# Attention and involution in one kernel: closing steps that wait for operand and bank, and a last chunk whose tap weights TensorE makes

## The chip, the cores and the metric

The kernel runs on one core of one Trainium2 chip. The core has TensorE (PE, matrix products into PSUM), VectorE (DVE), ScalarE (ACT), GpSimd (POOL) and SyncE (SP, which here only issues DMAs), each with its own instruction stream in a fixed order, and 16 DMA engines. An instruction that waits holds up all that stand behind it on its engine. The metric is the device time of one execution in microseconds.

## The reference

The input x is (4, 512, 64, 64) in float32. Two layers follow each other, each with its input added to its output.

```python
# layer 0: self-attention over the 4096 positions, 128 inner channels
q, k, v = wq x + bq, wk x + bk, wv x + bv
attn = softmax(q^T k)
x = wo (v attn^T) + bo + x
# layer 1: involution, 7 x 7 taps, groups of 16 channels
o1 = relu(s1 * (W1 x) + b1)                 # 512 -> 128 channels
w  = Ws relu(sr * (Wr o1) + br) + bs        # 128 -> 32 -> 8 groups x 49 taps
acc[c] = sum over taps of w[c // 16, tap] * o1[c] shifted by the tap
x = s3 * (W3 acc) + b3 + x                  # 128 -> 512 channels
```

## The kernel before

A batch (there are four) is worked in three kinds of stages. `keys_values` makes the keys and the transposed values of all 4096 positions. `attention` then takes 8 chunks of 512 queries; for each it runs through 32 tiles of 128 keys. In one such iteration PE makes a score tile `pss` for two iterations ahead, ACT takes its exponential into `pt`, PE adds `v` times `pt` to `po`, and DVE adds `pt` to `pacc` for the softmax sums. [...]

All else that a chunk needs is done by generators that the attention of the next chunks steps once an iteration, through `chores()`:

- `finish_chunk`: ACT copies `po` to `on`; PE spreads the sums over all partitions (`pl`); DVE takes four reciprocals `rl` (L327) and multiplies `on` by `rl` (L330); four matmuls `pwo` give the output projection, which DVE adds to the x chunk `xb` (L337); four matmuls into `p1` and ACT (L353) give `o1`; ACT adds b3 to `xb` (L365); `pr` and ACT (L371) give `red`, the 32 reduced channels repeated in four row groups; four matmuls `pc` of 32 rows each and ACT (L386) give `wc`, the 392 weights of the taps of every position. SP writes `wc` to a scratch in DRAM (`wsp`, L393). From there seven broadcast loads `wb` of 1792 KB (seven taps each; `pump`, L171) bring every group's weights to its 16 channels. The pool `wb` has three buffers, and at most two pieces are issued ahead.
- `involution`: for each of the 49 taps DVE multiplies the shifted `o1` (kept in PSUM as `po1`) by its weights (L215), and POOL adds the product to `acc` (L229). Products go to a pool of seven buffers. Taps from 28 on need rows of the next chunk's `o1` and wait until that is noted in `ready`.
- `close_chunk`: four matmuls `py` with W3, which DVE adds to `xb` (L246), and the store of the chunk (L252).

PSUM gives two banks to the tag `mm`, which `pl`, `pwo`, `p1`, `pr`, `pc`, `py` and `pq` share in turn; two to `pss` and `pk`; and one each to `po`, `pacc` and `po1`.

The order of the instructions is laid down when the kernel is built. A planner keeps a clock `pe` of the matmuls issued so far, and in `free` the time to which each other engine is booked. A generator that yields comes again in the next iteration, and the yields in `finish_chunk` and `close_chunk` are fixed in number. `pace()` meters the taps (0.70 a microsecond of `pe`), and a tap is held back while its piece, by the planner's figures (`PIECE_US` 7.4 a piece), has not landed, or while DVE or POOL is booked too far ahead. The framework's scheduler may then still move instructions on an engine.

After the last batch's attention comes the tail, where nothing is left to lay beside the steps: finishing, closing and taps are stepped three, three and two at a time. There PE takes a part of the additions: of the odd taps up to 45 it adds the product to `accp` by a matmul with the identity, and DVE adds `accp` to `acc` at the end (L232). A last check of the sums decides whether a general path, which doesn't run with these inputs, must compute everything again.

Of the kernel before, what the change touches and what calls it, by code (L numbers as in the profile page):

```python
# [8 lines left out]
F32 = mybir.dt.float32  # L9
# [40 lines left out]


PE_COLUMN = 0.43 / 256
DVE_OP, POOL_OP = 0.7, 1.28
PIECE_US, X_US, WC_US, LAND_US = 7.4, 3.8, 3.6, 3.5

SAFE = (1e-30, 1e20)

# [2 lines left out]
def fast_path(  # L60
# [46 lines left out]

    finishing, closing, taps = [], [], []  # L110
    pe = 0.0
    due, seen = 0.0, 0.0
    free = {"dve": 0.0, "pool": 0.0, "dma": 0.0}
    ready = set()
    pending, loaded = [], []

# [4 lines left out]
    def takes(engine, us):  # L121
        free[engine] = max(free[engine], pe) + us
        return free[engine]

    def load_x(kind, b, c):
        xt = xpool.tile([P, CT, CH], F32, tag="x", name=f"{kind}_{b}_{c}")
# [58 lines left out]
    def involution(b, c, o1):  # L185
        top = RW + PAD

        po1 = ps1.tile([P, RW + 2 * PAD, W + 2 * PAD], F32, tag="o1", name=f"po1_{b}_{c}")
        for _ in range(2):
            yield "wait"  # L190
        nc.scalar.copy(po1[:, :top], o1[:, :top])
        yield "wait"
        acc = work2.tile([P, RW, W], F32, tag="acc", name=f"acc_{b}_{c}")
        accp = None
        for tap in range(NTAP):
            dy, dx = divmod(tap, K)
            if dx == 0:
                if dy == PAD + 1:
                    while (b, c) not in ready:
                        yield "wait"  # L200
                    yield "wait"
                    nc.scalar.copy(po1[:, top:], o1[:, top:])
                    yield "wait"
                wb, landed = loaded.pop(0)
                pump()
            while "tail" not in ready and (
                pe < landed or free["dve"] > pe + 3.0 or free["pool"] > pe + 6.0
            ):
                yield "wait"
            free["pool"] = max(free["pool"], takes("dve", DVE_OP))  # L210
            takes("pool", POOL_OP)
            prod = acc
            if tap:
                prod = prods.tile([P, RW, W], F32, tag="prod", name=f"prod_{b}_{c}_{tap}")
            nc.vector.tensor_tensor(  # L215
                prod, po1[:, dy : dy + RW, dx : dx + W],
                wb[:, dx, :].rearrange("p (r w) -> p r w", r=RW), ALU.mult,
            )
            if tap and "tail" in ready and tap % 2 and tap < NTAP - 2:

                first = accp is None
                if first:
                    accp = ps1.tile([P, CH], F32, tag="po", name=f"accp_{b}_{c}")
                mm(
                    accp, ident, prod.rearrange("p r w -> p (r w)"),
                    start=first, stop=tap == NTAP - 4,
                )
            elif tap:
                nc.gpsimd.tensor_tensor(acc, acc, prod, ALU.add)  # L229
            yield  # L230
        if accp is not None:
            nc.vector.tensor_tensor(  # L232
                acc, accp.rearrange("p (r w) -> p r w", r=RW), acc, ALU.add
            )
        closing.append(close_chunk(b, c, acc))


    def close_chunk(b, c, acc):
        xt = xb[b, c]
        for _ in range(5):  # L240
            yield
        for t in range(CT):
            py = ps.tile([P, CH], F32, tag="mm", name=f"py_{b}_{c}_{t}")
            mm(py, w_slice(O_W3, t), acc.rearrange("p r w -> p (r w)"))
            takes("dve", DVE_OP)
            nc.vector.scalar_tensor_tensor(  # L246
                xt[:, t, :], py, v1(V_S3 + t), xt[:, t, :], ALU.mult, ALU.add
            )
            for _ in range(2):
                yield  # L250
        takes("dma", X_US)
        nc.sync.dma_start(out_r[b, :, :, c * CH : (c + 1) * CH], xt)  # L252
        del xb[b, c]
# [40 lines left out]
    def queries(b, c):  # L294
        xt = xb[b, c]
        pq = ps.tile([P, CH], F32, tag="mm", name=f"pq_{b}_{c}")
        for t in range(CT):
            mm(pq, w_slice(O_WQ, t), xt[:, t, :], t == 0, t == CT - 1)
        q = work2.tile([P, CH], F32, tag="q", name=f"q_{b}_{c}")
        nc.scalar.activation(q, pq, AF.Identity, bias=v1(V_BQ))  # L300
        return q

# [11 lines left out]
    def finish_chunk(b, c, o1s, po, sums):  # L314
        xt = xb[b, c]
        on = work2.tile([P, CH], F32, tag="on", name=f"on_{b}_{c}")
        nc.scalar.copy(on, po)
        for _ in range(3):
            yield
        pl = ps.tile([P, CH], F32, tag="mm", name=f"pl_{b}_{c}")  # L320
        mm(pl, ones, sums)
        rl = work1.tile([P, CH], F32, tag="rl", name=f"rl_{b}_{c}")
        for i in range(4):
            yield
            cols = slice(i * P, (i + 1) * P)
            takes("dve", 0.9)
            nc.vector.reciprocal(rl[:, cols], pl[:, cols])  # L327
        nc.sync.dma_start(rls[b * NCH + c : b * NCH + c + 1, :], rl[:1, :])
        takes("dve", DVE_OP)
        nc.vector.tensor_tensor(on, on, rl, ALU.mult)  # L330
        for _ in range(2):
            yield
        for t in range(CT):
            pw = ps.tile([P, CH], F32, tag="mm", name=f"pwo_{b}_{c}_{t}")
            mm(pw, w_slice(O_WO, t), on)
            takes("dve", DVE_OP)
            nc.vector.scalar_tensor_tensor(  # L337
                xt[:, t, :], pw, bo[:, t : t + 1], xt[:, t, :], ALU.add, ALU.add
            )
            yield  # L340
            if t % 2:
                yield
        p1 = ps.tile([P, RW, W], F32, tag="mm", name=f"p1_{b}_{c}")
        for t in range(CT):
            mm(
                p1.rearrange("p r w -> p (r w)"), w_slice(O_W1, t), xt[:, t, :],
                t == 0, t == CT - 1,
            )
            if t == 1:
                yield  # L350
        o1 = o1s[c]
        inner = o1[:, PAD : PAD + RW, PAD : PAD + W]
        nc.scalar.activation(inner, p1, AF.Relu, bias=v1(V_B1), scale=v1(V_S1))  # L353
        if c + 1 < NCH:
            o1s[c + 1] = new_o1(b, c + 1)
            nc.gpsimd.tensor_copy(  # L356
                o1s[c + 1][:, :PAD, PAD : PAD + W], o1[:, RW : RW + PAD, PAD : PAD + W]
            )
        if c > 0:
            nc.gpsimd.tensor_copy(  # L360
                o1s.pop(c - 1)[:, PAD + RW :, PAD : PAD + W], o1[:, PAD : 2 * PAD, PAD : PAD + W]
            )
        for t in range(CT):

            nc.scalar.activation(xt[:, t, :], xt[:, t, :], AF.Identity, bias=v1(V_B3 + t))  # L365
            if t % 2:
                yield
        pr = ps.tile([P, CH], F32, tag="mm", name=f"pr_{b}_{c}")
        mm(pr, wt[:, O_WR : O_WR + P], inner)
        red = work1.tile([P, CH], F32, tag="red", name=f"red_{b}_{c}")  # L370
        nc.scalar.activation(red, pr, AF.Relu, bias=v1(V_BR), scale=v1(V_SR))  # L371
        for _ in range(2):
            yield
        wc = work1.tile([P, 4, CH], F32, tag="wc", name=f"wc_{b}_{c}")
        for m0 in range(0, 4, 2):
            pcs = []
            for m in range(m0, m0 + 2):

                pc = ps.tile([P, CH], F32, tag="mm", name=f"pc_{b}_{c}_{m}")
                mm(  # L380
                    pc[:NWC, :], wt[CR * m : CR * (m + 1), O_WC : O_WC + NWC],
                    red[CR * m : CR * (m + 1), :], shared=2,
                )
                pcs.append(pc)
            for m, pc in zip(range(m0, m0 + 2), pcs):
                nc.scalar.activation(  # L386
                    wc[:NWC, m, :], pc[:NWC, :], AF.Identity,
                    bias=vec[:NWC, V_BC + m : V_BC + m + 1],
                )
            yield  # L390
        wsp = scratch.tile([4 * NWC, CH], F32, tag="wsp", name=f"wsp_{b}_{c}")
        written = takes("dma", WC_US) + LAND_US
        nc.sync.dma_start(wsp.rearrange("(m r) n -> r m n", m=4), wc[:NWC])  # L393
        pending.extend((wsp, written, i, f"wb_{b}_{c}_{i}") for i in range(NTAP // PIECE))
        pump()
        if c > 0:
            ready.add((b, c - 1))
        if c == NCH - 1:
            ready.add((b, c))
        taps.append(involution(b, c, o1))  # L400


    def attention(b, kt, vT):
# [5 lines left out]
        def score(n):  # L409
            c, j = divmod(n, nj)  # L410
            pss = ps.tile([P, CH], F32, tag="s", name=f"pss_{b}_{c}_{j}")
            mm(pss, kt[:, j * P : (j + 1) * P], qs[c])
            pt = ptpool.tile([P, CH], F32, tag="pt", name=f"pt_{b}_{c}_{j}")
            nc.scalar.activation(pt, pss, AF.Exp)  # L414
            pts[n] = pt

# [2 lines left out]
        for n in range(NCH * nj):  # L419
# [3 lines left out]
                paccs[c] = ps1.tile([P, CH], F32, tag="acc", name=f"pacc_{b}_{c}")  # L423
            if j == 14 and c + 1 < NCH:
                xb[b, c + 1] = load_x("xb", b, c + 1)
            if j == 8 and c == NCH - 1 and b + 1 < B:
                for i in range(2):
                    xa[b + 1, i] = load_x("xa", b + 1, i)
# [19 lines left out]
    for b in range(B):  # L448
        kv = keys_values(b)
        if b == 0:  # L450
# [3 lines left out]
                mm(pb[:, t : t + 1], w_slice(O_WO, t), v1(V_BVC))  # L454
            bo = const.tile([P, CT], F32, name="bo")
            nc.vector.tensor_tensor(bo, pb, vec[:, V_BO : V_BO + CT], ALU.add)
        attention(b, *kv)
    ready.add("tail")
    while finishing or closing or taps:
        step(finishing, 3)  # L460
        step(closing, 3)
        step(taps, 2)


    ok = const.tile([B * NCH, CH], F32, name="ok")
# [395 lines left out]
```

## Time and profile before

| what | us |
| --- | --- |
| median of three runs | 2900.23 |
| lowest and highest run | 2894.04, 2903.88 |
| the profiled execution's own time | 2898.7 |
| its span, first to last instruction | 2896.9 |
| PE busy | 2702.9 |
| DVE busy | 1919.7 |
| POOL busy | 1916.3 |
| ACT busy | 954.5 |
| last `po` matmul ends | 2760.5 |

The mean granted TensorE clock over the span was 0.972. The DMA engines moved 540.84 MB, of which the 224 pieces of `wb` are the most. In the lists below, a line of groups gives code line, engine, operation, destination and sources, shapes, count, then busy time and the mean ns of one, and the idle time before the group with what ended it. A line of a timeline gives start and duration in microseconds, and in brackets how long the engine had been idle and what released it.

### The profile page before, as it was taken

What the parts mean: (1) busy time and instruction counts of PE and PEld (TensorE: products, weight loads), DVE (VectorE), ACT (ScalarE), POOL (GpSimd) and SP (SyncE); (2) the same over time, 40 slices, a digit from 0 to 9 for tenths busy, and PEclk for the clock granted to TensorE, in tenths of its full rate; (3) what the DMA queues carried; (4) which work ended last, traced back from release to release, by engine and by line L of the source; (5) the groups of instructions that cost most, each with busy time, mean ns of one, the idle gap of its engine ahead of it and who ended that gap; (6) DMA issues with size and microseconds to landing.
All of it is one profiled execution on the core that took longest, in us unless ns stands there. A gap on an engine that the chain in (4) does not pass through costs nothing.

```text
span 2896.9 us, 23193 instructions
## 1 busy us (share of the span) xinstructions
PE 2702.9 (93%) x6250; PEld 1150.1 (40%) x6250; DVE 1919.7 (66%) x3016; ACT 954.5 (33%) x1569; POOL 1916.3 (66%) x1623
## 2 busy tenths in 40 slices
PE   8999999999899999999989999999989999999975
PEld 4444443343344444443434444443334444444421
DVE  0447777876456777777464777777636577777864
ACT  2333333332233333333223333333233333333310
POOL 0028877777734877887780777778865288777744
PEclk9999999999999999999999999999999999999987
DMA  6048888889937988888991989998895588888896
GB/s 213 15 100 180 205 202 194 202 200 226 237 84 183 198 199 202 199 202 203 253 215 41 213 199 207 204 202 206 213 242 139 123 201 201 201 189 189 188 229 167
DMA packets 97532, 540.84 MB, mean 187 GB/s; under 512 B 6640, under 2 KB 6768, under 8 KB 68592
## 3 DMA queue, kind: packets, MB, share of 16 engines
q1 hardware_dynamic: 97104, 538.01, 79.5%
q8 instruction: 51, 0.84, 0.1%
q10 hardware_dynamic: 288, 1.27, 0.1%
q14 instruction: 89, 0.73, 0.1%
HBM read 479.94 MB, written 59.24 MB: 186 GB/s over the span
## 4 chain that ended last, share of the span: by engine, by line
PE 37%; DMA 33%; POOL 14%; DVE 10%; issue 5%; ACT 1%; SPq 0%; POOLq 0%; DVEq 0%; ACTq 0%
DMA wb<-wsp 31%; POOL acc L229 13%; PE pss L147 11%; PE po L147 11%; PE py L147 4%; DVE pacc L439 4%; PE p L147 4%; DVE prod L215 3%; PE pwo L147 3%; DVE rl L327 2%; DMA wsp<-wc 2%; PE pv L147 1%; PE pk L147 1%; PE pq L147 1%; DMA out_dram<-xb 0%
## 5 line engine op out<-in xcount | busy, mean ns | idle before, releaser
L229 POOL TENSOR_TENSOR acc<-acc,prod 128x512 f32<-128x512 f32 x1488 | 1889.9, 1270 | 462.5 <-DVE prod L215 317.7
L215 DVE TENSOR_TENSOR prod<-po,wb 128x512 f32<-128x512 f32 x1536 | 1001.0, 681 | 281.5 <-DMA wb<-wsp 200.9
L147 PE MATMUL pss<-q,k 128*128 128x512 f32 x2048 | 1070.5, 605 | 34.5 <-ACT pt L414 34.5
L147 PE MATMUL po<-pt,v 128*128 128x512 f32 x2048 | 1063.0, 602 | 0.0
L414 ACT ACTIVATE pt<-pss 128x512 f32<-128x512 f32 x1024 | 610.5, 597 | 1255.1 <-PE pss L147 1128.4
L439 DVE TENSOR_TENSOR pacc<-pacc,pt 128x512 f32<-128x512 f32 x960 | 662.1, 690 | 289.9 <-ACT pt L414 287.1
L147 PEld LDWEIGHTS pss<-q,k 128*128 128x128 f32 x2048 | 387.2, 192 | 555.2 <-issue 485.0
L147 PEld LDWEIGHTS po<-pt,v 128*128 128x128 f32 x2048 | 393.0, 193 | 506.0 <-issue 487.9
L356 POOL COPY o<-o 128x192 f32<-128x192 f32 x28 | 9.7, 348 | 463.2 <-ACT o L353 317.4
L147 PE MATMUL pwo<-on,wt 128*128 128x512 f32 x256 | 143.1, 643 | 80.6 <-DVE on L330 78.3
L246 DVE SCALAR_TENSOR_TENSOR xb<-py,vec,xb 128x512 f32<-128x512 f32 x128 | 95.4, 745 | 100.5 <-PE py L147 99.7
L147 PE MATMUL py<-acc,wt 128*128 128x512 f32 x256 | 136.5, 620 | 22.1 <-DVE xb L337 12.1
L215 DVE TENSOR_TENSOR acc<-po,wb 128x512 f32<-128x512 f32 x32 | 22.1, 692 | 187.9 <-DMA wb<-wsp 187.8
L147 PE MATMUL pk<-xa,wt 128*128 128x512 f32 x256 | 122.7, 618 | 3.5 <-DMA xa<-x_dram 3.5
L365 ACT ACTIVATE xb<-xb,vec 128x512 f32<-128x512 f32 x128 | 91.9, 718 | 91.9 <-PE p L147 87.4
L147 PE MATMUL p<-xb,wt 128*128 128x512 f32 x256 | 120.1, 592 | 0.0
L147 PE MATMUL pv<-xa,wt 128*128 128x512 f32 x256 | 118.3, 600 | 0.0
L327 DVE RECIPROCAL rl<-pl 128x128 f32<-128x128 f32 x128 | 115.6, 929 | 1.6 <-PE pl L147 1.6
L147 PE MATMUL pq<-xb,wt 128*128 128x512 f32 x256 | 115.7, 592 | 0.0
L147 PEld LDWEIGHTS pwo<-on,wt 128*128 128x128 f32 x256 | 50.5, 207 | 160.2 <-DVE on L330 101.2
L386 ACT ACTIVATE wc<-pc,vec 98x512 f32<-98x512 f32 x128 | 81.2, 684 | 80.1 <-PE pc L147 80.1
L337 DVE SCALAR_TENSOR_TENSOR xb<-pwo,bo,xb 128x512 f32<-128x512 f32 x128 | 94.5, 740 | 14.8 <-PE pwo L147 14.5
(50 smaller groups left out, 822.2 us busy)
## 6 DMA issues: line engine op xcount, KB each, us to landing
wb<-wsp SPq DMA_DIRECT2D x224, 1792.0 KB
xa<-x_dram SPq DMA_DIRECT2D x32, 1024.0 KB
xb<-x_dram SPq DMA_DIRECT2D x32, 1024.0 KB
out_dram<-xb SPq DMA_DIRECT2D x32, 1024.0 KB
wsp<-wc SPq DMA_DIRECT2D x32, 784.0 KB
wt<-wts_dram ACTq DMA_DIRECT2D x1, 1137.0 KB
wt<-wts_dram SPq DMA_DIRECT2D x1, 512.0 KB
rls<-rl SPq DMA_DIRECT2D x32, 2.0 KB
```

The source lines that it names most:

```text
L147: nc.tensor.matmul(o, lhsT=lhsT, rhs=rhs, start=start, stop=stop)
L215: nc.vector.tensor_tensor(prod, po1[:, dy : dy + RW, dx : dx + W], wb[:, dx, :].rearrange("p (r w) -> p r w", r=RW), ALU.mult,)
L229: nc.gpsimd.tensor_tensor(acc, acc, prod, ALU.add)
L246: nc.vector.scalar_tensor_tensor(xt[:, t, :], py, v1(V_S3 + t), xt[:, t, :], ALU.mult, ALU.add)
L327: nc.vector.reciprocal(rl[:, cols], pl[:, cols])
L337: nc.vector.scalar_tensor_tensor(xt[:, t, :], pw, bo[:, t : t + 1], xt[:, t, :], ALU.add, ALU.add)
L356: nc.gpsimd.tensor_copy(o1s[c + 1][:, :PAD, PAD : PAD + W], o1[:, RW : RW + PAD, PAD : PAD + W])
L365: nc.scalar.activation(xt[:, t, :], xt[:, t, :], AF.Identity, bias=v1(V_B3 + t))
L386: nc.scalar.activation(wc[:NWC, m, :], pc[:NWC, :], AF.Identity, bias=vec[:NWC, V_BC + m : V_BC + m + 1],)
L414: nc.scalar.activation(pt, pss, AF.Exp)
L439: nc.vector.tensor_tensor(paccs[c], paccs[c], pt, ALU.add)
```

## The change

The planner's fixed yields in `finish_chunk`, `close_chunk` and `involution` give way to two conditions. `until(time)` yields until the planner's clock has reached a time, by which it reckons the operand to be ready. `bank()` does the same for the next bank of the tag `mm`: a list `banks` holds the times at which the two banks are reckoned to come free. ACT has an account of its own, and 0.3 us are reckoned for a hop between engines. In `finish_chunk` the b3 copies now stand behind `red`, the note in `ready` comes before the weights are made, and the four `pc` are laid down in two adjacent pairs.

The last chunk of the last batch has a way of its own, `involution_last`. It makes no `wc`, no scratch and no pieces. For each tap PE makes the weights of all 128 channels at once from 32 rows of `red` and a table `ws` into the two banks of `pss`; DVE adds the bias and multiplies by the shifted `o1` in one instruction; 33 of the products are added by PE through the identity into `accp`, and 15 by POOL. The table is loaded in batch 3 into one of the six buffers of the pool `x` and keeps it to the end. The tail runs the finishing to its end first, and then steps two taps of the last chunk for one of the chunk before it, all of whose additions are now POOL's.

```diff
-    free = {"dve": 0.0, "pool": 0.0, "dma": 0.0}
+    free = {"dve": 0.0, "pool": 0.0, "act": 0.0, "dma": 0.0}
+    banks = [0.0, 0.0]
...
+    def until(us, sign=None):
+        while pe < us and "tail" not in ready:
+            yield sign
+
+    def bank():
+        yield from until(banks[0])
+        banks.pop(0)
...
-            if tap and "tail" in ready and tap % 2 and tap < NTAP - 2:
...
-            elif tap:
+            if tap:
                 nc.gpsimd.tensor_tensor(acc, acc, prod, ALU.add)
...
+    def involution_last(b, c, o1, red):
+        acc = work2.tile([P, RW, W], F32, tag="acc", name="acc_last")
+        accp = ps1.tile([P, RW, W], F32, tag="po", name="accp")
+        by_pe = [tap for tap in range(1, NTAP - 4) if tap % 4]
+        late = []
+
+        def add(tap, prod):
+            if tap in by_pe:
+                mm(
+                    accp.rearrange("p r w -> p (r w)"), ident, prod.rearrange("p r w -> p (r w)"),
+                    tap == by_pe[0], tap == by_pe[-1],
+                )
+            else:
+                nc.gpsimd.tensor_tensor(acc, acc, prod, ALU.add)
+
+        for tap in range(NTAP):
+            r0 = CR * (tap % 4)
+            dy, dx = divmod(tap, K)
+            pw = ps.tile([P, RW, W], F32, tag="s", name=f"pw_{tap}")
+            mm(
+                pw.rearrange("p r w -> p (r w)"),
+                ws[r0 : r0 + CR, tap // 4 * P : (tap // 4 + 1) * P], red[r0 : r0 + CR, :],
+            )
...
+            nc.vector.scalar_tensor_tensor(
+                prod, pw, v1(V_BS + tap), o1[:, dy : dy + RW, dx : dx + W], ALU.add, ALU.mult
+            )
+            if tap:
+                late.append((tap, prod))
+            if len(late) > 2:
+                add(*late.pop(0))
+            yield
+        for tap, prod in late:
+            add(tap, prod)
+        nc.vector.tensor_tensor(acc, accp, acc, ALU.add)
+        closing.append(close_chunk(b, c, acc))
...
     def close_chunk(b, c, acc):
         xt = xb[b, c]
-        for _ in range(5):
-            yield
+        yield from until(free["pool"] + HOP_US)
         for t in range(CT):
+            yield from bank()
             py = ps.tile([P, CH], F32, tag="mm", name=f"py_{b}_{c}_{t}")
             mm(py, w_slice(O_W3, t), acc.rearrange("p r w -> p (r w)"))
-            takes("dve", DVE_OP)
+            banks.append(takes("dve", DVE_OP) + HOP_US)
...
     def finish_chunk(b, c, o1s, po, sums):
...
+        takes("act", ACT_OP)
         nc.scalar.copy(on, po)
-        for _ in range(3):
-            yield
+        yield from until(free["dve"] + HOP_US)
+        yield from bank()
         pl = ps.tile([P, CH], F32, tag="mm", name=f"pl_{b}_{c}")
...
+        banks.append(free["dve"] + HOP_US)
         nc.sync.dma_start(rls[b * NCH + c : b * NCH + c + 1, :], rl[:1, :])
-        takes("dve", DVE_OP)
         nc.vector.tensor_tensor(on, on, rl, ALU.mult)
-        for _ in range(2):
-            yield
+        yield from until(takes("dve", DVE_OP) + HOP_US)
         for t in range(CT):
+            yield from bank()
             pw = ps.tile([P, CH], F32, tag="mm", name=f"pwo_{b}_{c}_{t}")
             mm(pw, w_slice(O_WO, t), on)
-            takes("dve", DVE_OP)
+            banks.append(takes("dve", DVE_OP) + HOP_US)
...
+        if (b, c) == (B - 1, NCH - 1):
+            taps_last.append(involution_last(b, c, o1, red))
+            return
+        yield from until(made)
         wc = work1.tile([P, 4, CH], F32, tag="wc", name=f"wc_{b}_{c}")
...
+            if (b, c, j) == (B - 1, 5, 0):
+                nc.sync.dma_start(ws, wts[:, O_WS:])
...
+        if b == B - 1:
+            ws = xpool.tile([P, CT * CH], F32, tag="x", name="ws")[:, : NWT - O_WS]
         attention(b, *kv)
     ready.add("tail")
-    while finishing or closing or taps:
-        step(finishing, 3)
-        step(closing, 3)
-        step(taps, 2)
+    while finishing:
+        step(finishing, 1)
+        step(closing, 1)
+        step(taps, 1)
+    while closing or taps or taps_last:
+        step(taps_last, 2)
+        step(taps, 1)
+        step(closing, 1)
```

## The prediction

> **What bounds the kernel now.** I read the page's first part and its chain first, then the waits, then the timelines of one chunk in the steady part, and last the tail.
>
> Page, parts 1, 4 and 5 (busy us, share of the span, count; the chain's shares; a group's busy and mean ns, then the idle time before it):
> ```profile
> PE 2702.9 (93%) x6250; PEld 1150.1 (40%) x6250; DVE 1919.7 (66%) x3016; ACT 954.5 (33%) x1569; POOL 1916.3 (66%) x1623
> ...
> PE 37%; DMA 33%; POOL 14%; DVE 10%; issue 5%; ACT 1%; SPq 0%; POOLq 0%; DVEq 0%; ACTq 0%
> ...
> L229 POOL TENSOR_TENSOR acc<-acc,prod 128x512 f32<-128x512 f32 x1488 | 1889.9, 1270 | 462.5 <-DVE prod L215 317.7
> L215 DVE TENSOR_TENSOR prod<-po,wb 128x512 f32<-128x512 f32 x1536 | 1001.0, 681 | 281.5 <-DMA wb<-wsp 200.9
> ```
> PE is nearly full, yet DMA holds a third of the chain: it is a loop through several engines that sets the period. The waits (total, times, longest):
> ```profile
> DVE prod L215 <- DMA wb<-wsp: 200.9, 82, 7.4
> DVE acc L215 <- DMA wb<-wsp: 187.8, 31, 22.9
> ...
> PE pwo L147 <- DVE on L330: 78.3, 27, 3.6
> ```
> Timeline of DVE in one chunk (start, us, instruction, idle before it):
> ```profile
> 1982.32 0.69 DVE L215 TENSOR_TENSOR acc<-po,wb 128x512 f32<-128x512 f32 x1 [4.23 <-DMA wb<-wsp]
> ...
> 1990.91 0.69 DVE L215 TENSOR_TENSOR prod<-po,wb 128x512 f32<-128x512 f32 x1 [1.92 <-DMA wb<-wsp]
> ...
> 1999.46 0.69 DVE L215 TENSOR_TENSOR prod<-po,wb 128x512 f32<-128x512 f32 x1 [1.89 <-DMA wb<-wsp]
> ...
> 2001.27 1.76 DVE L327 RECIPROCAL rl<-pl 128x128 f32<-128x128 f32 x2
> ...
> 2006.41 0.68 DVE L330 TENSOR_TENSOR on<-on,rl 128x512 f32<-128x512 f32 x1
> ```
> and of PE:
> ```profile
> 2007.14 1.13 PE L147 MATMUL pwo<-on,wt 128*128 128x512 f32 x2 [2.87 <-DVE on L330]
> ...
> 2012.08 1.10 PE L147 MATMUL py<-acc,wt 128*128 128x512 f32 x2 [1.24 <-DVE xb L337]
> ```
> DVE works in the order that was laid down, so it sits at the first product of the third wb piece until that lands (1999.46); the reciprocals stand behind that product, `on` behind them, and PE at pwo behind `on`. The pieces land 8.6 us apart; 224 pieces took 1914 us of DMA time, 8.55 each. The loop closes: pwo to the issue of wsp 37.1 us (a PE stretch), to wb_0's issue 4.4, to the third landing 28.3, to pwo 7.7: 77.5 us, which is the period (77.3 to 79.4 in most chunks) against 72.2 us of PE work (84 matmuls by 0.86). The excess of chunks 1 to 6 sums to 131 us over the four batches. PE's other gaps: some 10 at the start, 26 in the three chunks 7, 57 at the three batch changes, 64 after 2760.
>
> In the tail, the 136.4 us from the last po (2760.5) to the end, DMA is the bound:
> ```profile
> 2856.80 4.28 DVE L215 TENSOR_TENSOR prod<-po,wb 128x512 f32<-128x512 f32 x7 [3.93 <-DMA wb<-wsp]
> 2864.94 4.28 DVE L215 TENSOR_TENSOR prod<-po,wb 128x512 f32<-128x512 f32 x7 [3.87 <-DMA wb<-wsp]
> 2872.91 4.28 DVE L215 TENSOR_TENSOR prod<-po,wb 128x512 f32<-128x512 f32 x7 [3.69 <-DMA wb<-wsp]
> 2880.42 0.69 DVE L232 TENSOR_TENSOR acc<-accp,acc 128x512 f32<-128x512 f32 x1 [3.23 <-POOL acc L229]
> ```
> Each piece feeds 4.28 us of products in 8 us; the end follows 16.5 us after 2880.4.
>
> **The change, part by part.** Sums go against the profiled execution, 2898.7 us (1.5 below the median, inside the runs). Orders are counted in the program as built.
>
> *1. The steady part.* The same matmuls, products and DMAs remain, and SP's order within a chunk is the same (wsp, five pieces, rls, two pieces, out), so only places move. I compare, from the end of a chunk's last pc, the PE work that stands ahead of a waiting matmul (room) with the time until its operand is there (need). Need begins with 34.7 us (pc end to landing of the third piece, as above), then DVE's instructions up to the operand: 0.60 a product or pacc by start-to-start distance, 0.65 an xb, 0.9 a reciprocal.
>
> Before, room to pwo is 45 matmuls by 0.86 = 38.7; need 34.7 + 7.7 = 42.4: short by 3.8. The py behind it is short by 1.4 more. 5.2 a chunk; the trace shows 5.7 on average in chunks 2 to 6. All chunks 1 to 6: 118 counted, 131 measured, ratio 1.11.
>
> After, pc stands 1.7 to 3.4 us nearer to the chunk's start (gain), but pwo stands 1 to 5 us later behind pl, and the closing py move ahead of pwo, because their planned wait for POOL is over soon. The planner still reckons 7.4 us a piece where 8.55 is measured, so it believes DVE free earlier than it is. Worked example, finish of chunk 2 with the closing of chunk 0: py_0_1 needs the bank that DVE's xb of py_0_0 empties, and that xb stands behind the third piece's first product. Room 36 matmuls = 31.0; need 34.7 + 3 by 0.60 + 0.9 + 0.65 = 38.1: short by 7.1. Chunk 3, by the same count: 5.6 (4.5 of it at py_1_1). In chunks 4 and 5 up to nine DVE instructions, not three, stand between the third piece and the reciprocals. Shortfalls over the batches, before to after: chunk 1 13.7 to 18.0, chunk 2 20.8 to 28.4, chunk 3 20.8 to 22.4, chunk 4 20.8 to 21.2, chunk 5 20.8 to 21.2, chunk 6 20.8 to 20.0, chunk 7 (three) 17.4 to 17.8. Chunks 1 to 6: 118 to 131, with the ratio 131 to 146: +15.
>
> Waits now come as one longer stop. The clock answers to that:
> ```profile
> core 0: us, PE busy (x), PEclk, DMA share, GB/s
> 1077.00:1080.40 3.40, 3.40 (x6) 0.61 0.97 202
> 2007.00:2010.40 3.40, 3.26 (x8) 1.00 1.00 211
> ```
> The first stretch follows a pwo wait of 3.50, the second one of 2.87: 0.61 of 3.4 us loses 1.3. Eight waits of 4.5 to 5.5 (chunks 2 and 3) lose perhaps half of that more than their counterparts, which are already gated at times: 8 by 0.7, less the part that later slack takes up: +2. I take **+17** (ends: +2 if the counting errs by its own 11% downwards on 131, +32 upwards).
> The Trainium skill, "TensorE: Matmul & The Clock Gate", Part 1, says that an idle window of about 3.4 us halves the clock for about as long; by it the eleven stops above 3.4 us in the table would each cost 1.7, 19 instead of 2, and the sum would be 2943. It speaks against gathering short waits into one; the trace has waits of 3.3 that kept the clock and one of 2.79 that lost it, so I keep the rows.
>
> *2. The accounts themselves* (until, bank, ACT's account, red before the xb+b3 copies, ready earlier) issue nothing. ACT is 33% busy and the four xb+b3 (0.72 each) leave the path to red; that is in the earlier pc above. Without that cover they would cost 2.9 a chunk.
>
> *3. Batch changes.* xb_1 no longer stands ahead of wb_7_0 on SP: the first pieces land one x load (3.2 us) earlier; but seven more products (7 by 0.60 = 4.2) stand ahead of the next pacc on DVE. Taken as 0; ends -3 and +3 each, -9 and +9.
>
> *4. ws and the x buffer.* One more 0.85 MB load (an x load of 1 MB: 3.2 us, so 2.7 of DMA) in batch 3, and five x buffers left: xb_6 waits for out_1, xb_7 for out_2, both issued some 60 us ahead of need. 0, at worst +2.7.
>
> *5. The tail.* Gone: wsp_7 and seven pieces (60 us of DMA), four pc. New order: nothing but the finish first. From the last po, at the tail's own distances (pl 2.5, four reciprocals 3.4, on, four pwo, four p1, pr), pw_0 starts after about 17.8. Then 49 pw, 33 adds and the four py of chunk 5 on PE: 86 by 0.86 = 74; two 32-row matmuls side by side cost 1.1 not 1.72 (pc: four records in 1.10), there are 12 such pairs: 74 - 7.4 = 66.6. With hand-offs (each add waits for DVE, each pw for one of two banks) 71. Meanwhile DVE takes up chunk 6 only one product for two pw, so that POOL, which now has all 48 adds of chunk 6 (before, PE had 23 of them), has 30 still to do when the last pw is done: 30 by 1.33 = 40, alone. Then 15.8 from ready acc to the end, as before, plus 3 to the first of the 30: 17.8 + 71 + 3 + 40 + 15.8 = 148 against 136.4: **+11**. Low end: POOL never idle from pw_0 on (5 adds of chunk 5, 15 of chunk 7, 48 of chunk 6, 68 by 1.33 = 90): 17.8 + 3 + 90 + 15.8 = 126.6, -10. High end: PE at the 0.79 that the clock averaged from 2797 to 2881: 71/0.79 = 90, +30.
>
> Sum: 2898.7 + 17 + 0 + 0 + 11 = 2926.7; I say **2926**.
>
> **The rivals.**
> - *Both effects cancel* (2885 to 2905, middle 2895). Products brought forward in the steady part pay back what is lost at py, and POOL never idles in the tail: 0 to +5, and -10. For: 1.7 to 3.4 us earlier pc. Against: the count above, which met the old excess within 11%.
> - *The stops vanish* (the other side). If wb_2 came before PE needs it, the shortfall at pwo and py would go. Place: DVE's first product of the third piece. It decides once two pieces land some 2.3 us earlier (8.55 to the planned 7.4 each) or the pc gain of up to 3.4 is not eaten. Half of 131 saved: 2898.7 - 65 + 11 = 2845. Against: DMA share is 0.97 to 1.00 in these windows, and DMA bytes are unchanged.
> - *Worse*: all ends high, the gate after each long stop and in the tail: +32 and +25: about 2955. For: the clock row and 30 POOL adds in a row. Against: PE is dense in the pw phase.
> - That the change does nothing is excluded: its orders differ in every chunk.
>
> **How the numbers follow.** Forecast 0.55 (own range 2905 to 2950); cancel 0.15; vanish 0.10; worse 0.20. The range leaves out the vanishing case and the upper third of the worse one: 2888 to 2957. Bound for a change that a measurement tells: 0.3%, 8.7 us. Faster: 0.10 and a quarter of cancelling, 0.14; same: most of the rest of cancelling, 0.10; slower 0.76.
>
> **What will show it.** Right, if: PE waits at py on xb (chunks 2 and 3) of 4 us and more appear and waits at pwo on `on` shrink; periods of chunks 1 to 6 average about 0.7 us more; POOL ends with some 30 adds of chunk 6 in one row, and last po to end is near 148. Wrong, if the DVE waits for wb fall clearly, or the pw phase takes under 60 us, or POOL's last adds run beside it.

## The result, and the profile after

The changed kernel takes 3026.65 us (median; 3022.11 to 3031.05) against 2902.06 for the kernel before in the same comparison (2894.04 to 2904.86): a ratio of 1.0434, 95% interval 1.0405 to 1.0463. It is 125 us slower, where 26 us were forecast. The direction was right; the size, and with it the range up to 2957, was not.

The page of the changed kernel, parts 1 and 5 (busy us and share; a group's busy and mean ns, then its idle time before and the main releaser). The line numbers have moved: L147, L215, L246, L330, L337 and L442 of before are L157, L223, L282, L368, L375 and L497 here.

```profile
PE 2778.7 (92%) x6310; PEld 1162.4 (38%) x6310; DVE 1933.3 (64%) x3014; ACT 947.7 (31%) x1563; POOL 1933.5 (64%) x1638
...
L157 PE MATMUL py<-acc,wt 128*128 128x512 f32 x248 | 142.9, 664 | 98.6 <-DVE xb L282 47.2
L157 PE MATMUL pwo<-on,wt 128*128 128x512 f32 x256 | 141.1, 636 | 63.6 <-DVE on L368 43.0
```

The same two groups before:

```profile
L147 PE MATMUL pwo<-on,wt 128*128 128x512 f32 x256 | 143.1, 643 | 80.6 <-DVE on L330 78.3
...
L147 PE MATMUL py<-acc,wt 128*128 128x512 f32 x256 | 136.5, 620 | 22.1 <-DVE xb L337 12.1
```

PE's waits at pwo shrank, and those at py grew by more. Of the 98.6 us at py, 36.4 are a single wait at the end of the tail, for POOL's last add; the rest lies mostly before the tail. The waits of before for `on` (78.3 us) have partly become waits for the bank that DVE's xb empties.

The last po ends at 2801.2 us, 40.7 later than before, and the end comes 220.5 us after it instead of 136.4. So 84.1 us of the loss lie in the tail and 40.7 in what comes before it. Within the second part I use one measure for all kernels below: the time between the starts of successive 512-column matmul records (a matmul leaves two: the 1024 score tiles have 2048) beyond the 0.43 us from one record to the next at full clock, summed from one chunk's last pc to the next chunk's. By what is finished in that stretch, it is:

| PE's lost time, us | batch changes (3) | chunk 1 (4) | chunks 2 to 6 (20) | chunk 7 (3) | last po to end |
| --- | --- | --- | --- | --- | --- |
| before | 57.1 | 17.5 | 113.5 | 25.9 | 136.4 |
| after | 66.1 | 26.6 | 134.4 | 28.3 | 220.5 |

Of the 21 us in chunks 2 to 6, chunk 2 has 14.1 and chunk 3 has 5.3. Timeline of PE there, changed kernel (start, us, idle before it):

```profile
1704.57 1.02 PE L157 MATMUL py<-acc,wt 128*128 128x512 f32 x2
...
1712.43 2.08 PE L157 MATMUL py<-acc,wt 128*128 128x512 f32 x2 [5.12 <-DVE xb L282]
1714.30 1.79 PE L157 MATMUL pss<-q,k 128*128 128x512 f32 x2
```

and of DVE in the same stretch:

```profile
1709.06 0.69 DVE L223 TENSOR_TENSOR prod<-po,wb 128x512 f32<-128x512 f32 x1 [1.92 <-DMA wb<-wsp]
...
1710.86 0.94 DVE L365 RECIPROCAL rl<-pl 128x128 f32<-128x128 f32 x1
1711.72 0.65 DVE L282 SCALAR_TENSOR_TENSOR xb<-py,vec,xb 128x512 f32<-128x512 f32 x1
```

That is the forecast's worked example: the second py needs a bank that the first py's xb empties, and the xb stands behind the first product of the third piece, which lands at 1709. The forecast's text gives 4.5 to 5.5 us for such stops, and its sum for this one 7.1; measured 5.12, with a wait of 1.05 at pl ahead of it. The first records after it last twice as long; the clock in the windows after two such stops:

```profile
core 0: us, PE busy (x), PEclk, DMA share, GB/s
1712.00:1715.40 3.40, 2.97 (x4) 0.56 1.06 223
1799.00:1802.40 3.40, 3.40 (x5) 0.50 1.08 232
```

The tail shows what nobody had counted. Timeline of PE, changed kernel:

```profile
2821.21 2.73 PE L157 MATMUL pw<-red,ws 32*128 32x512 f32 x4 [0.84 <-DVE acc_last L260]
2823.86 2.08 PE L157 MATMUL accp<-prod_last,ident 128*128 128x512 f32 x2
2825.87 2.07 PE L157 MATMUL pw<-red,ws 32*128 32x512 f32 x2
...
2859.12 1.88 PE L157 MATMUL py<-acc,wt 128*128 128x512 f32 x4
2863.30 1.09 PE L157 MATMUL pw<-red,ws 32*128 32x512 f32 x2 [2.30 <-DVE prod_last L260]
```

and the windows of the tail:

```profile
core 0: us, PE busy (x), PEclk, DMA share, GB/s
2806.00:2819.00 13.00, 11.00 (x18) 0.79 0.00 0
2824.00:2849.00 25.00, 25.00 (x30) 0.50 0.11 28
2853.00:2863.00 10.00, 8.00 (x19) 1.00 0.12 24
2866.00:2958.00 92.00, 91.01 (x108) 0.50 0.22 51
```

PE is busy without a gap, and yet runs at half its clock for 25 us. It recovers behind the first py of chunk 5 (2849.8), stays at full clock while the other three pass, waits 2.30 us, and is at half for the remaining 92. At half clock each matmul, or pair of pw side by side, takes 2.0 us. The phase from the first pw to the end of the last takes 139 us where 71 were forecast. After it POOL adds on alone, as forecast:

```profile
2968.85 34.81 POOL L228 TENSOR_TENSOR acc<-acc,prod 128x512 f32<-128x512 f32 x26 [0.71 <-DVE prod L223]
```

The tail by the forecast's own terms, forecast and measured: pw_0 17.8 and 18.0 after the last po; the phase 71 and 138.6; to the last POOL add 43 and 45.8; to the end 15.8 and 18.0.

### The profile page after: what moved, and what is told of

Read it like the earlier page. It is cut to its first block, busy times and chain, and to the rows that moved or that the text cites. A ratio compares the mean times of both kernels' runs of the same rounds, so it can differ in the third digit from the quotient of the medians.

```text
span 3021.7 us, 23314 instructions
## 1 busy us (share of the span) xinstructions
PE 2778.7 (92%) x6310; PEld 1162.4 (38%) x6310; DVE 1933.3 (64%) x3014; ACT 947.7 (31%) x1563; POOL 1933.5 (64%) x1638
## 5 line engine op out<-in xcount | busy, mean ns | idle before, releaser
L223 DVE TENSOR_TENSOR prod<-po,wb 128x512 f32<-128x512 f32 x1488 | 967.8, 681 | 286.2 <-DMA wb<-wsp 187.7
L157 PE MATMUL pss<-q,k 128*128 128x512 f32 x2048 | 1071.6, 606 | 33.4 <-ACT pt L467 33.4
L157 PE MATMUL po<-pt,v 128*128 128x512 f32 x2048 | 1055.8, 598 | 0.5 <-ACT on L355 0.4
L157 PEld LDWEIGHTS pss<-q,k 128*128 128x128 f32 x2048 | 390.3, 193 | 558.3 <-issue 493.0
L157 PEld LDWEIGHTS po<-pt,v 128*128 128x128 f32 x2048 | 392.0, 192 | 507.3 <-issue 488.2
L157 PE MATMUL py<-acc,wt 128*128 128x512 f32 x248 | 142.9, 664 | 98.6 <-DVE xb L282 47.2
L157 PE MATMUL pwo<-on,wt 128*128 128x512 f32 x256 | 141.1, 636 | 63.6 <-DVE on L368 43.0
L282 DVE SCALAR_TENSOR_TENSOR xb<-py,vec,xb 128x512 f32<-128x512 f32 x128 | 94.8, 741 | 56.9 <-PE py L157 55.4
L157 PE MATMUL pk<-xa,wt 128*128 128x512 f32 x256 | 122.6, 618 | 2.1 <-DMA xa<-x_dram 2.1
L223 DVE TENSOR_TENSOR acc<-po,wb 128x512 f32<-128x512 f32 x31 | 21.4, 692 | 159.9 <-DMA wb<-wsp 159.6
L157 PE MATMUL p<-xb,wt 128*128 128x512 f32 x256 | 120.7, 594 | 0.0
L157 PE MATMUL pv<-xa,wt 128*128 128x512 f32 x256 | 117.4, 594 | 0.0
L157 PE MATMUL pq<-xb,wt 128*128 128x512 f32 x256 | 115.7, 592 | 0.0
L157 PEld LDWEIGHTS py<-acc,wt 128*128 128x128 f32 x248 | 48.6, 205 | 169.0 <-DVE xb L282 60.8
L375 DVE SCALAR_TENSOR_TENSOR xb<-pwo,bo,xb 128x512 f32<-128x512 f32 x128 | 94.9, 743 | 28.4 <-PE pwo L157 27.9
```

The lines of the kernel that those rows point to most:

```text
L157: nc.tensor.matmul(o, lhsT=lhsT, rhs=rhs, start=start, stop=stop)
L223: nc.vector.tensor_tensor(prod, po1[:, dy : dy + RW, dx : dx + W], wb[:, dx, :].rearrange("p (r w) -> p r w", r=RW), ALU.mult,)
L282: nc.vector.scalar_tensor_tensor(xt[:, t, :], py, v1(V_S3 + t), xt[:, t, :], ALU.mult, ALU.add)
L375: nc.vector.scalar_tensor_tensor(xt[:, t, :], pw, bo[:, t : t + 1], xt[:, t, :], ALU.add, ALU.add)
```

## Experiments

Two theories stood at the start. *Stages:* the two losses are separate, one in the order of py, one in the tail's clock. *Coupling:* one follows from the other, for instance the table load or the five buffers slow batch 3, or the new steps leave the tail in a bad state. All ratios are to the kernel before on the same chip.

### Is it the 32 rows that keep the clock down?

```diff
-                ws[r0 : r0 + CR, tap // 4 * P : (tap // 4 + 1) * P], red[r0 : r0 + CR, :],
+                ws[:, tap // 4 * P : (tap // 4 + 1) * P], red,
```

> The changed kernel, but each pw matmul contracts all 128 rows of red and of the table's slot instead of 32; the same 49 matmuls, adds and waits in the same order. The weights of four taps are summed in each pw, so the output is not the reference's. Theory A (matmuls over 32 rows, alternating with whole ones, keep the TensorE clock at half: 0.52 from 2863 to 2958): the clock goes to about 1.0, the phase from pw_0 to the last pw falls from 139 us to 75 to 90, the kernel to some 2965 to 2980 us. Theory B (the hand-offs between PE and DVE, one add waiting for each product, keep it at half): no change, 3020 to 3030 us. Theory C (the 4.28 us wait ahead of pwo gated the clock, and nothing opens it again in so broken a row): no change either, and the clock at half from 2806 on.

Measured: 2965.68 us (two runs), ratio 1.0210, interval 1.0162 to 1.0258. The phase took 77.2 us, the tail 161.1. The window over the phase:

```profile
core 0: us, PE busy (x), PEclk, DMA share, GB/s
2819.00:2895.00 76.00, 73.70 (x171) 1.00 0.36 87
```

The order is the same, the wait of 4.28 us ahead of pwo is there, and so is one of 2.30 in the middle of the phase; the clock stays at 1.00. (The short wait of 0.84 behind the first two pw is gone, as whole ones do not run side by side.) Theories B and C fall: neither the hand-offs nor the early wait alone hold it down. In this order the rows decide.

### The tail undone

The last-chunk path, its table and its loop are taken out; the tail of before stands in their place.

```diff
-        if (b, c) == (B - 1, NCH - 1):
-            taps_last.append(involution_last(b, c, o1, red))
-            return
...
-            ws = xpool.tile([P, CT * CH], F32, tag="x", name="ws")[:, : NWT - O_WS]
```

> The changed kernel with the tail of before: no last-chunk path, no table, the last chunk's weights through scratch and pieces, odd taps of the tail added by PE. The changed steps and their order up to the last po stay. If the two stages add up as the two traces say (last po to end 220.5 us after, 136.4 before), this is 84 us less than the changed kernel: 2940 to 2946 us, still 40 us over before. If the steady part loses time only because of the table load and the five x buffers in batch 3, it is near 2902. If the tail of before suffers from the new steps, above 2950.

Measured: 2946.22 us, ratio 1.0146 (1.0110 to 1.0183). The last po ends at 2798.4, the tail takes 141.0. So the loss before the tail is that of the changed steps, and the table load with its buffer has little to do with it: 2798.4 without against 2801.2 with it, about the 2.7 us that the forecast gave at most.

### The tail alone

The kernel before, with `involution_last`, its table and the new loop, and the early return in `finish_chunk`.

> The kernel before with only the last-chunk path and its tail: fixed yields and accounts as before. If the stages add up: 2902 + 84 = 2980 to 2990 us, and last po to end near 220 us. If the slow tail needs the new steps, near 2902.

Measured: 2918.11 us, ratio 1.0044 (1.0026 to 1.0062), a loss of 13 us and not of 84. The expectation was wrong: the tail takes 153.2 us, its phase 75.1, and all its pw still have 32 rows:

```profile
core 0: us, PE busy (x), PEclk, DMA share, GB/s
2791.00:2864.00 73.00, 72.81 (x164) 1.00 0.35 84
```

The same mix of 32-row and whole matmuls runs for 73 us at full clock. So it is not too little work for the full clock as such. The difference lies at the entry: here whole matmuls (py and p) follow the last long wait (7.98 us at 2784), and py of chunk 5 and pw then stand close together with no wait between them,

```profile
2789.95 1.02 PE L147 MATMUL py<-acc,wt 128*128 128x512 f32 x2
2790.98 1.13 PE L147 MATMUL pw<-red,ws 32*128 32x512 f32 x4
2792.03 1.13 PE L147 MATMUL py<-acc,wt 128*128 128x512 f32 x2
```

while the changed kernel enters with waits of 0.88, 0.87 and 0.84 us around two pairs of pw. The theory became: the mix of 32-row and whole matmuls keeps an open clock open, but does not open a closed one. So the two parts do not add up: alone they cost 41 and 13 us, together 125. Some 70 us come only where the new steps and the new tail meet, and *Stages* falls for the tail.

### The clock held by whole matmuls

Eight matmuls of 128 rows are added, whose result nobody reads; `filler` issues them into a bank that is free in the tail.

```diff
+            if tap == 1:
+                filler(4, red)
+            if tap == 15:
+                filler(4, late[-2][1].rearrange("p r w -> p (r w)"))
             yield
```

> The changed kernel with eight added matmuls of 128 rows whose result nobody reads: four between pw_1 and pw_2, four between the last py of chunk 5 and pw_16, the two places where PE waits 0.8 and 2.3 us just before the clock falls. All pw stay at 32 rows. Theory A (matmuls over 32 rows hold an open clock but cannot open a closed one; the waits close it): with the waits filled the clock stays at 1.0 through the phase, which falls from 139 us to some 78 to 85, and the kernel to 2965 to 2985 us. Rival (32-row matmuls alternating with whole ones are too little work for the full clock in themselves, and the run with the steps of before only happened to escape): the clock falls again within a few us after each group of fillers, 3020 us or more.

Measured: 2972.12 us (two runs), ratio 1.0221 (1.0192 to 1.0251), 55 us less than the changed kernel although PE has more to do. The tail takes 168.0 us, the phase 86.7 with the fillers in it, and the clock over it is 1.00:

```profile
core 0: us, PE busy (x), PEclk, DMA share, GB/s
2825.00:2910.00 85.00, 82.44 (x186) 1.00 0.33 77
```

The second group did not even fill its wait. It came behind it:

```profile
2856.39 3.70 PE L157 MATMUL warm<-prod_last,ident 128*128 128x512 f32 x8 [2.21 <-DVE prod_last L264]
2860.02 1.12 PE L157 MATMUL pw<-red,ws 32*128 32x512 f32 x2
2861.07 1.12 PE L157 MATMUL accp<-prod_last,ident 128*128 128x512 f32 x2
```

The wait is nearly as long as the one after which the changed kernel fell to half for the rest of the phase (2.21 against 2.30 us); 3.7 us of whole matmuls behind it were enough. Which of the waits closes the clock in the changed kernel was not taken apart.

### The planner's figure for a piece

On top of the run with the tail of before:

```diff
-PIECE_US, X_US, WC_US, LAND_US = 7.4, 3.8, 3.6, 3.5
+PIECE_US, X_US, WC_US, LAND_US = 8.6, 3.8, 3.6, 3.5
```

> The changed kernel with the tail of before and one figure of the planner changed: a piece is reckoned at 8.6 us, as measured, not 7.4. If the wrong figure is why py is laid down before DVE can have emptied its bank (the prediction's reason), the waits of 4 to 5 us at py in chunks 2 and 3 go and this is 15 to 35 us faster than the run with the tail of before alone. By the count of the built order only 3 us of the 149 us of shortfall go (py_0_1 of chunk 2 is still 4.9 short, py_1_1 of chunk 3 still 4.5): then it is within 8 us of that run, and the reason is not the figure.

Measured: 2934.27 us, ratio 1.0113 (1.0070 to 1.0157), 12 us less than the run without it, which lies between the two forecasts; the two intervals overlap. And it is not where the forecast's reason would have it: chunks 2 and 3 lose 35.3 and 26.4 us (35.9 and 27.0 without), and chunks 2 to 6 together 141.2 against 132.1. The gain is at the batch changes (32.2 against 67.6), and chunk 7 gives back 14 (40.5 against 26.7). PE's waits for xb at py did not shrink either: 56.9 us in 17 waits, against 46.5 in 11 without it. The figure is not why py stands too early; it settles how many taps are left when a batch ends.

### py held behind pwo

On top of the run with the tail of before; `projecting` is filled when a finish begins and cleared after its four pwo.

```diff
         yield from until(free["pool"] + HOP_US)
+        while projecting and "tail" not in ready:
+            yield
         for t in range(CT):
```

> The run with the tail of before, and one condition added to the planner: the closing py of a chunk are not laid down while a finish has not yet issued its four pwo. If the steady part loses because py stands ahead of pwo and needs a bank that DVE empties only after the third piece (the forecast's reason), the waits of 4 to 5.5 us at py in chunks 2 and 3 and the half-clock stretches behind them go. Counted shortfall over the 27 chunks falls from 149 us to 107, under the 135 of the kernel before: 2895 to 2910 us, against 2946 without the condition. If the loss has another source (DMA contention, the accounts' other reorderings, DVE's extra products), it stays above 2930.

Measured: 2905.78 us, ratio 1.0008 (0.9993 to 1.0022): 40 us less than without the condition. Chunks 2 to 6 lose 81.2 us instead of 132.1, under the 113.5 of before. Waits of PE in this run (total, times, longest):

```profile
PE pwo L158 <- DVE on L346: 47.4, 22, 5.7
...
PE py L158 <- DVE xb L259: 17.8, 3, 6.2
```

Three waits for xb at py are left, against eleven of 47.2 us in the changed kernel. That the order of py cost what chunks 2 to 6 lost is shown. But the whole is no faster than before: batch changes lose 72.0 (57.1 before), chunk 1 31.6 (17.5). The three waits stand at the batch changes, where no finish is under way, so that the condition says nothing:

```profile
1505.44 2.08 PE L158 MATMUL py<-acc,wt 128*128 128x512 f32 x2 [6.24 <-DVE xb L259]
```

and on DVE it is the same picture, an xb behind products that wait for a piece:

```profile
1501.05 1.29 DVE L225 TENSOR_TENSOR prod<-po,wb 128x512 f32<-128x512 f32 x2 [4.66 <-DMA wb<-wsp]
...
1504.65 0.74 DVE L259 SCALAR_TENSOR_TENSOR xb<-py,vec,xb 128x512 f32<-128x512 f32 x1
```

### All repairs together

The condition on py, and a last-chunk path in which pw contracts 128 rows of a copy of red that is zero outside its own 32; one tap of each of the last two chunks in turn; every third product of chunk 6 added by PE into the free bank of pacc.

```diff
-                ws[r0 : r0 + CR, tap // 4 * P : (tap // 4 + 1) * P], red[r0 : r0 + CR, :],
+                ws[:, tap // 4 * P : (tap // 4 + 1) * P], rm[:, tap % 4, :],
...
-        step(taps_last, 2)
+        step(taps_last, 1)
```

> All repairs together: the condition on py; the last-chunk path with each pw over 128 rows, of which three groups of red are zero, so the weights are exact; the last two chunks stepped one tap to one, and of chunk 6 every third product added by PE into a second bank. Tail: pw_0 18.5 us after the last po, then 101 matmuls by 0.86 = 87, 7 for the last five POOL adds, 16 to the end: 128 to 132 us against 136 before. With the steady part of the run with the condition alone: some 5 us less than that run, 2870 to 2905 us. If the clock halves here too, the tail is above 180 us and the kernel near 2950.

Measured: 2902.52 us, ratio 0.9993 (0.9978 to 1.0007). The clock held (1.00 from 2800 to 2860) and the phase took 89.9 us, where 87 were reckoned, but the tail 138.9 and not 128 to 132. The last products of chunk 6 stand between the xb of chunk 7 on DVE, and the two closings run one after the other with their own waits: from the last pw to the end 31 us, not 23.

### Condition and figure, and the figure on the kernel before

The run with the condition, and the kernel before, each with 8.6 for 7.4.

> The changed steps with the tail of before, the condition on py, and the piece reckoned at 8.6 us. With the condition alone the steady chunks 2 to 6 gained 32 us on the kernel before (excess 81 against 114), and the batch changes and chunk 1 gave back as much (104 against 75); the figure of 8.6 alone took 35 us from the batch changes. If the two add up, the counted shortfall is 73 us (107 with the condition alone, 135 before): 2840 to 2880 us. If the late taps that the figure brings only move the wait to the end of the batch (chunk 7 rose by 14 us with the figure alone), 2890 to 2910.

> The kernel before with nothing but the piece reckoned at 8.6 us. The counted shortfall falls from 135 to 101 us. If the figure is worth something without the change: 2865 to 2890 us. If it needs the accounts of the change, 2895 to 2910.

Measured: 2897.48 us, ratio 0.9968 (0.9947 to 0.9989), for the first, and 2922.28, ratio 1.0059 (1.0039 to 1.0079), for the second. Neither did what the count of shortfalls promised; the first lies in its own second range, the second above both of its ranges. In the first the batch changes cost 36.2 us and the last po ends at 2732.2, 28 earlier than before; but the tail takes 158.5. In the second chunks 2 to 6 rise to 128.8 and chunk 7 to 43.1 while the batch changes fall to 29.3. Taps put off in one place are met in another.

### The version that beats both

All repairs and the figure 8.6.

> The run with all repairs, and the piece reckoned at 8.6 us. The run with the condition and 8.6 reached the last po 28 us earlier than the kernel before (2732 against 2760), but its tail was 22 us longer (158.5), since more taps were left over and all their pieces go through the DMA engines. The last-chunk path needs no pieces for its 49 taps. If the longer tail is the DMA engines' (pieces 8 us apart), it shrinks to 140 to 150 us here: 2872 to 2885 us, faster than both kernels. If it is POOL's and DVE's backlog, it stays near 158 or grows: 2890 to 2900.

Measured: 2884.43 us (2878.05 to 2888.59) against 2898.15, ratio 0.9951 (0.9935 to 0.9967). The last po ends at 2726.2, and the tail takes 149.9, inside the 140 to 150 expected: 8.6 less than with pieces for the last chunk. It is 0.5% faster than the kernel before.

| PE's lost time, us | batch changes | chunk 1 | chunks 2 to 6 | chunk 7 | last po to end |
| --- | --- | --- | --- | --- | --- |
| tail of before | 67.6 | 27.5 | 132.1 | 26.7 | 141.0 |
| steps of before | 54.1 | 16.8 | 116.0 | 26.4 | 153.2 |
| figure 8.6 | 32.2 | 22.7 | 141.2 | 40.5 | 146.3 |
| condition | 72.0 | 31.6 | 81.2 | 27.8 | 139.5 |
| all repairs | 70.7 | 31.7 | 79.3 | 27.7 | 138.9 |
| condition and 8.6 | 36.2 | 25.0 | 93.7 | 31.8 | 158.5 |
| before with 8.6 | 29.3 | 22.0 | 128.8 | 43.1 | 139.4 |
| all repairs and 8.6 | 41.5 | 24.8 | 85.5 | 29.4 | 149.9 |

## Why the prediction was right or wrong

**The steady part: the exchange right, two waits left out.** The count gave +13 us for chunks 1 to 6, to which the ratio and the clock brought it to +17; measured 30 (134.4 + 26.6 against 113.5 + 17.5). The stops at py came where the count put them (4.5 to 5.5 us forecast; 5.12 measured at chunk 2, 4.08 at chunk 3). PE over chunks 1 to 6 of the four batches, before:

```profile
core 0: us, PE busy (x), PEclk, DMA share, GB/s
180.70:647.80 467.10, 445.71 (x1028) 0.98 0.87 198
881.10:1346.30 465.20, 443.63 (x1030) 0.99 0.89 204
1578.20:2042.30 464.10, 443.58 (x1030) 0.99 0.89 204
2275.20:2740.00 464.80, 446.26 (x1030) 0.98 0.87 197
```

and after:

```profile
core 0: us, PE busy (x), PEclk, DMA share, GB/s
175.50:649.90 474.40, 447.71 (x1036) 0.99 0.85 194
886.50:1361.70 475.20, 446.85 (x1036) 0.99 0.87 199
1595.70:2071.90 476.20, 451.08 (x1034) 0.98 0.87 199
2305.70:2780.00 474.30, 447.07 (x1036) 0.99 0.86 195
```

The time in which PE stands idle there grew by 25 us, from 82.0 to 107.4, and the clock is no lower than it was: by the clock's record in the traces these chunks hold 58.0 us at 0.50 before and 54.6 after. So the term that came out too small is the +15 for the waits. Those at py for xb rose from 10.0 to 44.4 us and those at pwo for `on` fell from 70.7 to 24.3, as forecast. But two other waits, which the forecast does not name, came up with them: at pwo for the bank that DVE's xb empties (none to 20.6) and at pl for the sums (1.1 to 12.2). In the whole execution they were, before,

```profile
PE pl L147 <- DVE sums L442: 3.5, 3, 2.4
...
PE pwo L147 <- DVE xb L337: 2.2, 2, 2.0
```

and after

```profile
PE pwo L157 <- DVE xb L375: 19.1, 10, 2.9
...
PE pl L157 <- DVE sums L497: 12.2, 11, 3.4
```

The clock's term of +2 was not far off. In chunks 2 and 3, of 19.4 us more lost, 13.9 are waits; the 5.5 left are what the forecast's eight by 0.7 comes to before it takes off later slack. All eight stops there are followed by a stretch at 0.50, but so were six of the eight waits of 2.6 to 3.6 us at pwo that they replace. The Trainium skill's rule, which the forecast weighed and set aside ("TensorE: Matmul & The Clock Gate", Part 1: an idle window of some 3.4 us halves the clock for about as long), gave an estimate of 19 for the stops of the changed kernel alone. It fits those stops; it does not tell which of the shorter waits of before lost the clock as well (2.65 us at 375.0 did, 3.21 at 1233.3 did not), and so the difference between the kernels stayed small. The 3.21 is also the longest wait of before that kept the clock, where the forecast wrote 3.3.

**Its reason was half wrong.** The forecast laid the early py to the planner's 7.4 us a piece. With 8.6 the stops stayed; with py held behind pwo they went and 40 us with them. So py ahead of pwo is the cause, and the figure is not.

**Batch changes: taken as 0 with ends of 9; measured +9.0.** That is its upper end. Chunk 7 rose by 2.4 against 0.4.

**The tail: the failed step.** "71" for the pw phase, and with it "High end: PE at the 0.79". At full clock the size was nearly right: the phase takes 75.1 us with the steps of before and 77.2 with whole matmuls. The way to it was partly luck: the forecast added 0.86 a matmul and some time for hand-offs, but with the steps of before PE hardly waits, and each place of the alternation takes 1.05 us. And the changed kernel ran the phase at 0.50 for all but some 16 of its 139 us. The high end came from a mean over a stretch of before in which waits and work alternate, and a mean is no upper bound for a stretch that can stay in the lower state. At half clock the phase is 74 places (86 matmuls, each of the 12 pairs counted once) by 2.0 us, 148: with that end the range would have reached past 3000. The other terms of the tail stood within 3 us each. Why the clock closed is shown as far as the rows and the order go; which wait closes it stays open.

**The rivals.** That the stops vanish was refuted for the change. With the condition on py chunks 1 to 6 lose 112.8 us, against 131.0 in the kernel before: 18 less, where the rival had half of 131, and not because pieces came earlier: DVE's waits for wb rose from 388.7 us in all to 454.4. The rival "worse" named the cause, the clock in the tail, but priced it at 19 us (71 to 90) where 68 came. "PE is dense in the pw phase", given as evidence against it, was true and worth nothing: density in time did not open the clock.

## What to carry to other kernels

When one long wait takes the place of short ones, count the half-clock stretches of both orders: here waits of 2.6 to 3.6 us had one behind them six times in eight, stops of 4 to 5 us every time. And when the order of matmuls that share two banks changes, count the wait of each of them, also those that did not wait before. Where a new phase has matmuls over a part of the rows, ask in which clock state it is entered and what in it would open the clock again; where it can be entered closed, either contract all rows with zeros or put a few whole matmuls behind the wait, and let the half clock be the upper end of the estimate. A matmul whose bank is emptied by an engine with an order laid down in advance waits for all that stands ahead there: move it behind the transfers that are due, not only behind its own operand.

## What the runs showed of the hardware that was not expected

A mix of 32-row and 128-row matmuls, issued without gaps, ran 92 us at a granted clock of 0.50 in the changed kernel and 73 us at 1.00 in the kernel with the steps of before. With 128 rows throughout the clock was 1.00 after waits of 4.28 and 2.30 us as in the changed kernel, and 3.7 us of whole matmuls behind a wait of 2.21 us were enough to keep the mix at 1.00 to its end. Alternating between 32 and 128 rows cost 1.05 us a matmul at full clock, where whole ones follow each other in 0.86. Ahead of the tail, waits of 2.65 and 2.71 us (at 375.0 and 2704.6 in the kernel before) were followed by a stretch at 0.50, and one of 3.40 us (at 212.4 in the changed kernel) was not; of 3.48 us and more, all were in these two traces, but for the first wait of each execution.
